# Local attention on Trainium2: query and value blocks laid out anew, two norms behind the evacuations, the last division in another bank

## The chip, the cores and the metric

The kernel runs on one core of a Trainium2 chip (trn2). The metric is the device time of one execution in microseconds, the median of several runs. Engine names are those of the profile: PE (TensorE, matrix multiply), PEld (its weight loads), DVE (VectorE), ACT (ScalarE), POOL (GpSimd), SP (the engine that issues most DMAs).

## The reference

Four layers are applied, one after the other, to an input `x` of shape (4, 56, 56, 128), each as `x = x + layer(group_norm(x))`. Layer 0 holds everything that the change touches: a local attention over windows of 7 x 7 pixels, then an attention over the whole image, then a two-layer perceptron. Shortened:

```python
# layer 0, on the group-normed x
xs = roll(x, (-3, -3))                       # shifted windows
wins = window_partition(xs)                  # (4*64, 49, 128)
x = roll(window_reverse(mha(wins)), (3, 3))  # local attention: 4 heads of 32
xf = x.reshape(4, 56*56, 128)
xf = xf + mha(layernorm(xf))                 # attention over the image
h = gelu(layernorm(xf) @ w1 + b1)
xf = xf + (h @ w2 + b2)
# mha: q, k, v = x@wq+bq, x@wk+bk, x@wv+bv per head;
#      softmax(q k^T / sqrt(32)) v, then @ wo + bo
```

Layer 1 is an edge network with 56 nodes in each row, layer 2 a spectral (Fourier) attention over all images with its own convolutions, layer 3 a convolution along one axis with sums along the other. All data are float32.

## The kernel before, in words

The program takes the four images one after the other through layers 0 and 1: `fast_layer` for layer 0, then `edge_layer`. While image b is in its local attention, steps of layer 2's norms for image b - 1 are strewn in between (not in image 0). After image 3, layers 2 and 3 are done for all images together.

Channels lie on the 128 partitions and the 3136 pixels of an image on the free axis, in the order of the windows: 64 windows of 49 pixels (`WIN`). The local attention, `fast_windows`, works in eight groups `g` of eight windows (`N` = 392 columns). One group passes through these stages:

- `norm`: the group-normed input of the group, `w_xg`. ACT makes it for groups 0 and 1 (L368), DVE for the others (L193, through `apply_norm`).
- `project`: TensorE multiplies `w_xg` with the query, key and value weights into three PSUM banks (L375, L376, L380; the value product separately for the four pairs of windows and the two windows, "parities", of a pair). Then the banks are emptied: queries head by head into `w_qd`, DVE for heads 0 and 2 (L225) and ACT for heads 1 and 3 (L223), keys by ACT into `w_kT` (L383), values by DVE for parity 0 (L232) and by ACT for parity 1 (L230) into `w_vd`.
- `score`: one matmul for each window multiplies its keys with the queries of all four heads (L394). `w_qd` is zero outside each head's 32 partitions, so that the four heads come apart. An exponential on ACT follows (L397), into `w_pT`.
- `value`: matmuls with `w_vd` (L409) give the weighted values, and in a 33rd column, which holds ones, the sum for the division (L412, L413).
- `turn`, `output`, `central`, `variance`: transposition, output weights, and the centring and squares of the next layer norm.

Three sets of the buffers `w_xg`, `w_kT`, `w_qd`, `w_vd`, `w_pT` rotate. They are cleared once an image by POOL, set by set: the tail of `w_xg` (L339), `w_qd` (L340), the tails of `w_kT` and `w_pT` (L341, L342), `w_vd` (L343) and the column of ones in `w_vd` (L345); the ones of a set come after the L340 of the next set.

PE, ACT and DVE follow the order in which the Python code issues their instructions, so the loop of `fast_windows` is the schedule. POOL's order is left to the framework. In turn n of the loop, the stages run for groups n + 2, n, n - 1 and so on: the norm of a group stands ahead of the projection of the group before the last, on DVE's queue too.

At the end of the eight groups come the layer norm's root and reciprocal (`root`, `invert`), the division `divide` (a matmul that spreads the inverse, L460, and a multiply on DVE, L461) and `attended`, which makes queries, keys (L468, L469) and values (L477, L479) of the attention over the image. Here `bank()` gives PSUM banks from two tags in turn, `w_mm` (three banks) and `w_late` (tag "acc", two banks), steered by the count `turns`. What is left of `divide` and `attended` runs inside the next stage, whose eight PSUM banks are one tile `f_pm`; its first scores go to banks 0 to 3 (L827), followed by exponentials (L830).

Of the kernel before, what the change touches and what calls it, by code (L numbers as in the profile page):

```python
# [12 lines left out]
F32 = mybir.dt.float32  # L13
# [6 lines left out]
P = 128  # L20
# [5 lines left out]
WIN = 49  # L26
# [6 lines left out]
def bc(ap, axis, n):  # L33

    ap = ap.unsqueeze(axis)
    shape = list(ap.shape)
    shape[axis] = n
    return ap.to_broadcast(shape)
# [181 lines left out]
def evac(k, i, out, ps, bias):  # L220

    if i % 2:
        k.nc.scalar.activation(out, ps, AF.Identity, bias=bias)  # L223
    else:
        k.nc.vector.tensor_scalar_add(out, ps, bias)  # L225


def copy(k, i, out, ps):
    if i % 2:
        k.nc.scalar.copy(out, ps)  # L230
    else:
        k.nc.vector.tensor_copy(out, ps)  # L232
# [74 lines left out]
def fast_windows(k, w, xw, xf, mr, shift, beside, Q, K, V, h1, inverse):  # L307
# [9 lines left out]
    nc, tc = k.nc, k.tc  # L317
    scale = 1.0 / math.sqrt(32.0)
    heads = [slice(32 * h, 32 * h + 32) for h in range(4)]
    halves = [slice(0, 64), slice(64, P)]  # L320
    N = 8 * WIN
# [4 lines left out]
    with ExitStack() as es:  # L326
        big = es.enter_context(tc.tile_pool(name="w_big", bufs=1))
# [5 lines left out]
        for i in range(BUFS):  # L333
            xg = big.tile([P, N + 16], F32, name="w_xg%d" % i)
            kT = big.tile([P, N + 16], F32, name="w_kT%d" % i)
            qd = big.tile([P, 8, 4, WIN], F32, name="w_qd%d" % i)
            vd = big.tile([P, 4, 4, 2, 33], F32, name="w_vd%d" % i)
            pT = big.tile([P, 16 * WIN + 16], F32, name="w_pT%d" % i)
            nc.gpsimd.memset(xg[:, N:], 0.0)  # L339
            nc.gpsimd.memset(qd, 0.0)  # L340
            nc.gpsimd.memset(kT[:, N:], 0.0)  # L341
            nc.gpsimd.memset(pT[:, 16 * WIN:], 1.0)  # L342
            nc.gpsimd.memset(vd, 0.0)  # L343
            for par in range(2):
                nc.gpsimd.memset(vd[halves[par], :, :, par, 32], 1.0)  # L345
            fixed.append((xg, kT, qd, vd, pT))
        outs, columns, squares, roots, chunk = {}, {}, {}, {}, 0
        eps = big.tile([P, 1], F32, name="w_eps")
# [2 lines left out]
        turns = 0  # L351

        def bank():
            nonlocal turns
            if source:
                return source[0]()
            turns += late
            if turns % 2:
                return psum.tile([P, 512], F32, tag="acc", name="w_late")
            return psum.tile([P, 512], F32, tag="mm", name="w_mm", bufs=3)  # L360
# [11 lines left out]
        def project(g):  # L372
            xg, kT, qd, vd, pT = fixed[g % BUFS]
            pq, pk, pv = bank(), bank(), bank()
            nc.tensor.matmul(pq[:, :N], w.wq, xg[:, :N], start=True, stop=True)  # L375
            nc.tensor.matmul(pk[:, :N], w.wk, xg[:, :N], start=True, stop=True)  # L376
            for i in range(4):
                for par in range(2):
                    t = (2 * i + par) * WIN
                    nc.tensor.matmul(pv[halves[par], i * P:(i + 1) * P], xg[:, t:t + 64], w.wv, start=True, stop=True)  # L380
            for h in range(4):
                evac(k, h, qd[heads[h], :, h, :], pq[heads[h], :N].rearrange("p (w t) -> p w t", t=WIN), w.bq[heads[h]])
            nc.scalar.activation(kT[:, :N], pk[:, :N], AF.Identity, bias=w.bk)  # L383
            for par in range(2):
                copy(k, par, vd[halves[par], :, :, par, 0:32],
                     pv[halves[par]].rearrange("p (a h d) -> p a h d", a=4, h=4))

        def score(g):
            xg, kT, qd, vd, pT = fixed[g % BUFS]
            ss = psum.tile([P, 2, 512], F32, tag="ss", name="w_ss", bufs=1)  # L390
            for i in range(4):
                for par in range(2):
                    v = 2 * i + par
                    nc.tensor.matmul(ss[halves[par], i // 2, i % 2 * 4 * WIN:(i % 2 + 1) * 4 * WIN],  # L394
                                     kT[:, v * WIN:v * WIN + 64], qd[:, v].rearrange("p h t -> p (h t)"),
                                     start=True, stop=True)
            nc.scalar.activation(pT[:, :16 * WIN].rearrange("p (a n) -> p a n", a=2), ss[:, :, :8 * WIN], AF.Exp,  # L397
                                 scale=scale, bias=k.wkeys)

        def value(g):  # L400
            xg, kT, qd, vd, pT = fixed[g % BUFS]
            o = wk.tile([P, 2, 2, 4, 32], F32, name="w_o", bufs=3)
            for a in range(2):
                po = psum.tile([P, 4, 2, 33], F32, tag="acc", name="w_po")
                for h in range(4):
                    for pp in range(2):
                        i = 2 * a + pp
                        c = (4 * i + h) * WIN
                        nc.tensor.matmul(po[halves[pp], h].rearrange("p b d -> p (b d)"), pT[:, c:c + 64],  # L409
                                         vd[:, i, h].rearrange("p b d -> p (b d)"), start=True, stop=True)  # L410
                rec = wk.tile([P, 4, 2], F32, name="w_rec")
                nc.vector.reciprocal(rec, po[:, :, :, 32])  # L412
                nc.vector.tensor_mul(o[:, a].rearrange("p b h d -> p h b d"), po[:, :, :, 0:32], bc(rec, 3, 32))  # L413
            outs[g] = o
# [33 lines left out]
        def root(i):  # L448
            nc.scalar.activation(inverse[:, i, :], roots[i][:, :N], AF.Sqrt, scale=1024.0, bias=eps)
            step(True)  # L450

        def invert(i):
            nc.vector.reciprocal(inverse[:, i, :], inverse[:, i, :])
# [31 lines left out]
        def step(root):  # L485
            nonlocal root_next
            if begun and (root or not root_next):
                root_next = next(steps, None) == "root"

        def run(*stages):  # L490
            for stage, g in stages:
                if 0 <= g < NG:
                    stage(g)
                    step(False)
# [4 lines left out]
        begun = False  # L499
        for n in range(NG + 1):  # L500
            begun = n > 1
            run((norm, n + 2), (project, n), (score, n - 1), (value, n - 2), (turn, n - 3), (output, n - 4),
                (central, n - 5), (variance, n - 6))
        variance(3)
        root(0)
        run((value, 7), (turn, 6), (output, 5), (central, 4))
        late = True
        run((turn, 7))
# [4 lines left out]
            pass  # L513
        root(1)
        nc.scalar.activation(eps, k.eps, AF.Exp)
        run((attended, 1), (divide, 2))
        invert(1)
        for _ in steps:
# [105 lines left out]
def fast_layer(k, w, xw, xf, x1, st, beside, mr, shift):  # L624
# [9 lines left out]
    with ExitStack() as es:  # L634
# [4 lines left out]
        oT = big.tile([P, TOK], F32, name="f_oT")  # L639
        inverse = big.tile([P, 2, 8 * WIN], F32, name="f_inverse")  # L640
        use = fast_windows(k, w, xw, xf, mr, shift, beside, qT, kT, va, oT, inverse)

        ring = es.enter_context(tc.tile_pool(name="f_ring", bufs=1)).tile([P, RING, NB], F32, name="f_ring")
# [2409 lines left out]
```

## Time and profile before

| what | value |
|---|---|
| time, median of 3 runs | 3447.18 us (3444.64 to 3448.79) |
| the profiled execution: time, span | 3464.64 us, 3462.8 us |
| mean granted TensorE clock | 0.991 |
| PE busy | 96% |
| DVE, ACT, POOL busy | 77%, 62%, 37% |
| local attention of images 0, 1, 2, 3 starts at (first L368) | 46.83, 676.60, 1310.80, 1946.98 us |
| first L830 after it | 118.22, 752.40, 1388.39, 2023.26 us |

The profile is of one execution, which the profiler makes slightly longer than the median. A row of the timeline has the start in us from the span's start, the duration, engine, line, operation, the program's tile names (output, then inputs), the shapes and the number of instructions merged into the row; in brackets stands how long the engine had been idle and what ended that. A float32 matmul appears as two records. PE's busy time counts pipelined matmuls whose ends are modelled, so that 96% does not mean that it runs at its peak.

### The profile page before, as it was taken

To read this page: it belongs to the slowest core of one execution; us is meant where nothing else is said; L and a number is where in the kernel's file an instruction comes from. 1 tells how busy PE (TensorE), PEld (TensorE's weight loads), DVE (VectorE), ACT (ScalarE), POOL (GpSimd) and SP (SyncE) were. 2 spreads that over 40 slices of the span, in tenths; PEclk is the share of its full clock that TensorE was granted. 3 is DMA by queue.
4 is the path that set the end of the run, shared out by engine and by line. 5 is a ranking of instruction groups with operands and counts; after the bars stand their busy time and mean duration, and the time that the engine had idled before them with its cause. 6 is when DMAs were issued, how large, how long until landed. Compare 5 with 4: busy or idle time off the path is not lost. (4 is left out here: it accounts for less than half of the span.)

```text
span 3462.8 us, 64536 instructions
## 1 busy us (share of the span) xinstructions
PE 3337.5 (96%) x27834; PEld 1441.2 (42%) x27834; DVE 2659.6 (77%) x2552; ACT 2134.9 (62%) x2257; POOL 1284.9 (37%) x795
## 2 busy tenths in 40 slices
PE   7999999999999999999999999999999999999998
PEld 4433333353333435333343443333337443346664
DVE  6588867868888696788859858887785878886756
ACT  4688876668888575788857568887654012215432
POOL 1000017700000490000019400001785978875766
PEclk9999999999999999999999999999999999999989
DMA  2243420024434000444310034342113057742201
GB/s 106 46 94 86 97 54 19 20 58 87 97 86 86 19 1 20 110 99 94 89 41 1 20 82 93 89 97 54 38 36 85 1 124 182 182 110 80 61 10 56
DMA packets 97868, 243.42 MB, mean 70 GB/s; under 512 B 64440, under 2 KB 69816, under 8 KB 92440
## 3 DMA queue, kind: packets, MB, share of 16 engines
q0 software_dynamic: 16128, 102.77, 14.8%
q1 hardware_dynamic: 74728, 123.61, 12.2%
q10 hardware_dynamic: 6720, 12.85, 1.3%
q8 instruction: 220, 3.60, 0.4%
q14 instruction: 72, 0.59, 0.1%
HBM read 79.43 MB, written 31.33 MB: 32 GB/s over the span
## 5 line engine op out<-in xcount | busy, mean ns | idle before, releaser
L830 ACT ACTIVATE f_ring<-f_pm 128x1792 f32<-128x1792 f32 (+1 forms) x764 | 1093.8, 1482 | 226.7 <-PE f_pm L827 179.2
L682 DVE TENSOR_TENSOR f_acc<-f_acc,f_ring 128x1792 f32<-128x1792 f32 x468 | 947.5, 2025 | 190.8 <-ACT f_ring L830 160.0
L827 PE MATMUL f_pm<-f_qT,f_kT 32*128 32x448 f32 x5376 | 722.8, 571 | 9.9 <-ACT f_p L716 4.1
L693 PE MATMUL f_pm<-f_ring,f_va 128*32 128x448 f32 (+1 forms) x6304 | 589.4, 490 | 0.0
L672 POOL DMA_DIRECT2D f_far<-f_ring x112 | 96.5, 862 | 1328.2 <-ACT f_ring L830 1027.0
L1275 POOL TENSOR_TENSOR e_tp<-e_a,e_c 128x1792 f32<-128x1792 f32 (+2 forms) x172 | 480.4, 2839 | 33.5 <-issue 33.4
L1273 DVE TENSOR_TENSOR e_td<-e_a,e_pc 128x1792 f32<-128x1792 f32 (+2 forms) x292 | 478.3, 1704 | 8.8 <-ACT e_c L1261 8.8
L827 PEld LDWEIGHTS f_pm<-f_qT,f_kT 32*128 32x128 f32 x5376 | 260.1, 183 | 411.8 <-ACT f_ring L830 301.1
L693 PEld LDWEIGHTS f_pm<-f_ring,f_va 128*32 128x32 f32 x6304 | 163.8, 109 | 410.1 <-issue 397.8
L1277 ACT ACTIVATE e_tp<-e_tp 128x1792 f32<-128x1792 f32 (+2 forms) x172 | 253.3, 1495 | 98.0 <-POOL e_tp L1275 98.0
L2040 DVE TENSOR_TENSOR u_ud<-u_px,u_d 112x1792 f32<-112x1792 f32 x144 | 263.4, 1863 | 39.9 <-PE u_po L2045 35.6
L2042 POOL TENSOR_TENSOR u_up<-xh,u_d 112x1792 f32<-112x1792 f32 (+1 forms) x72 | 240.9, 3374 | 56.0 <-PE u_po L2045 42.8
L1344 PE MATMUL e_acc<-e_td,t_edge 128*32 128x448 f32 x1952 | 231.6, 542 | 6.6 <-DVE e_td L1273 6.4
L2045 PE MATMUL u_po<-u_ud,AT 112*64 112x448 f32 x1056 | 212.4, 541 | 0.5 <-DVE u_ud L2040 0.5
L1344 PE MATMUL e_acc<-e_tp,t_edge 128*32 128x448 f32 x1184 | 148.0, 543 | 23.7 <-ACT e_tp L1277 23.6
L2045 PEld LDWEIGHTS u_po<-u_ud,AT 112*64 112x64 f32 x1056 | 74.0, 137 | 126.5 <-issue 112.3
L1344 PEld LDWEIGHTS e_acc<-e_td,t_edge 128*32 128x32 f32 x1952 | 61.8, 110 | 142.4 <-issue 94.2
L737 DVE RECIPROCAL f_den<-f_den 128x448 f32<-128x448 f32 x28 | 82.6, 2951 | 44.9 <-ACT f_den L734 44.9
L1874 POOL TENSOR_TENSOR q_u<-iS,q_g 128x1792 f32<-128x1792 f32 x32 | 104.3, 3287 | 12.2 <-PE q_acc L1889 12.2
L813 POOL TENSOR_TENSOR x<-xf,xw 128x343 f32<-128x343 f32 x28 | 25.5, 909 | 221.5 <-DVE xf L802 221.5
L2145 ACT COPY x_ev<-x_po 56x896 f32<-56x896 f32 x32 | 28.8, 900 | 126.7 <-DMA x_xs<-xat 57.8
L1889 PE MATMUL q_acc<-q_u,S 64*64 64x448 f32 x1024 | 101.2, 539 | 2.1 <-DVE y L1908 1.1
(538 smaller groups left out, 4622.3 us busy)
## 6 DMA issues: line engine op xcount, KB each, us to landing
f_far<-f_ring POOLq DMA_DIRECT2D x112, 896.0 KB, 6.4
u_d<-dd SPq DMA_DIRECT2D x46, 784.0 KB
f_far<-f_ring SPq DMA_DIRECT2D x28, 896.0 KB
xw<-in_x SPq DMA_DIRECT2D x4, 1568.0 KB
x2d<-x SPq DMA_DIRECT2D x4, 1568.0 KB
xat<-x SPq DMA_DIRECT2D x4, 1568.0 KB
x_xs<-xat ACTq DMA_DIRECT2D x32, 196.0 KB
xm<-x_ev ACTq DMA_DIRECT2D x64, 98.0 KB
```

Source lines behind the costliest of these rows:

```text
L682: nc.vector.tensor_add(e.acc, e.acc, slots(j, c))
L693: nc.tensor.matmul(e.po[heads[h], part], va[o, c, heads[h]], p, start=(c == 0), stop=(c == 23 and part.stop == NB))
L827: nc.tensor.matmul(ss[:, i, :NB], kT[heads[h], c * P:(c + 1) * P], qT[heads[h], blk(j)], start=True, stop=True)
L830: nc.scalar.activation(ring[:, slot:slot + m, :], ss[:, :m, :NB], AF.Exp, scale=scale)
L1273: nc.vector.tensor_tensor(t, am, cm, ALU.max)
L1275: nc.gpsimd.tensor_sub(t, am, cm)
L1277: nc.scalar.activation(tf, tf, AF.Relu)
L1344: nc.tensor.matmul(acc[quarters[r0 + r], :NB], w.S[:, 0, :], t[:, r].rearrange("p l n -> p (l n)"), start=(g == 0), stop=(g == len(turns) ...
L1874: nc.gpsimd.tensor_mul(u, bc(st.iS[:, bp, c, :HH], 1, HEADS), bc(g[:, n, c, :], 2, HH))
L2040: nc.vector.tensor_mul(u, bc(px[:, :, :NB], 2, m), dm)
L2042: nc.gpsimd.tensor_mul(u, bc(x, 2, m), dm)
L2045: nc.tensor.matmul(po[64 * b2:64 * b2 + 64, :NB], st.AT[:, 8 * i + h0 + q, 2 * bp + b2, :], u[:, b2, q, :], start=(left == 16), stop=(left ...
```

## The change

Four things are changed, all in `fast_windows`.

- `w_qd` has its heads outermost, (4 heads, 8 windows, 49) instead of (8, 4, 49). A head's evacuation then writes one unbroken run of 392 columns, and a window's score matmul reads four runs of 49.
- `w_vd` has its parities outermost, (2, 4, 4, 33) instead of (4, 4, 2, 33). The value matmul reads two runs of 33 instead of one of 66.
- In turns 0 and 1 of the loop, `project(n)` comes ahead of `norm(n + 2)`. On DVE, the norms of groups 2 and 3 then stand behind the evacuations of groups 0 and 1.
- `turns` is raised by one after `root(1)`, so that in `attended(1)` and `divide(2)` the tags `w_mm` and `w_late` change places. The last division's bank is then `w_late`'s bank 6 instead of `w_mm`'s bank 1.

No instruction is added or dropped.

```diff
-            qd = big.tile([P, 8, 4, WIN], F32, name="w_qd%d" % i)
-            vd = big.tile([P, 4, 4, 2, 33], F32, name="w_vd%d" % i)
+            qd = big.tile([P, 4, 8, WIN], F32, name="w_qd%d" % i)
+            vd = big.tile([P, 2, 4, 4, 33], F32, name="w_vd%d" % i)
...
-                nc.gpsimd.memset(vd[halves[par], :, :, par, 32], 1.0)
+                nc.gpsimd.memset(vd[halves[par], par, :, :, 32], 1.0)
...
-                evac(k, h, qd[heads[h], :, h, :], pq[heads[h], :N].rearrange("p (w t) -> p w t", t=WIN), w.bq[heads[h]])
+                evac(k, h, qd[heads[h], h], pq[heads[h], :N].rearrange("p (w t) -> p w t", t=WIN), w.bq[heads[h]])
             nc.scalar.activation(kT[:, :N], pk[:, :N], AF.Identity, bias=w.bk)
             for par in range(2):
-                copy(k, par, vd[halves[par], :, :, par, 0:32],
+                copy(k, par, vd[halves[par], par, :, :, 0:32],
                      pv[halves[par]].rearrange("p (a h d) -> p a h d", a=4, h=4))
...
-                    nc.tensor.matmul(ss[halves[par], i // 2, i % 2 * 4 * WIN:(i % 2 + 1) * 4 * WIN],
-                                     kT[:, v * WIN:v * WIN + 64], qd[:, v].rearrange("p h t -> p (h t)"),
+                    nc.tensor.matmul(ss[halves[par], i // 2, i % 2 * 4 * WIN:(i % 2 + 1) * 4 * WIN].rearrange("p (h t) -> p h t", h=4),
+                                     kT[:, v * WIN:v * WIN + 64], qd[:, :, v, :],
                                      start=True, stop=True)
...
-                        nc.tensor.matmul(po[halves[pp], h].rearrange("p b d -> p (b d)"), pT[:, c:c + 64],
-                                         vd[:, i, h].rearrange("p b d -> p (b d)"), start=True, stop=True)
+                        nc.tensor.matmul(po[halves[pp], h], pT[:, c:c + 64], vd[:, :, i, h, :], start=True, stop=True)
...
-            run((norm, n + 2), (project, n), (score, n - 1), (value, n - 2), (turn, n - 3), (output, n - 4),
+            run(*((norm, n + 2), (project, n))[::-1 if n < 2 else 1], (score, n - 1), (value, n - 2), (turn, n - 3), (output, n - 4),
                 (central, n - 5), (variance, n - 6))
...
         root(1)
         nc.scalar.activation(eps, k.eps, AF.Exp)
+        turns += 1
         run((attended, 1), (divide, 2))
```

## The prediction

> **What bounds the kernel now.** I read the page first, then the timeline around the first microseconds of each image's window stage, engine by engine, then the waits of that stretch, then the granted clock in short windows. The page says that TensorE is busy all the time:
>
> ```profile
> span 3462.8 us, 64536 instructions
> ...
> PE 3337.5 (96%) x27834; PEld 1441.2 (42%) x27834; DVE 2659.6 (77%) x2552; ACT 2134.9 (62%) x2257; POOL 1284.9 (37%) x795
> ```
>
> That share is an average. The change lies in the window stage alone, which runs four times for about 72 us, so what counts is which wait ends last there. Image 1, DVE's timeline (start, duration, engine, line, operation; in brackets the idle time before and its releaser):
>
> ```profile
> 677.20 3.61 DVE L193 TENSOR_SCALAR w_xg<-xw,mr 128x392 f32<-128x392 f32 x1
> 680.73 0.60 DVE L225 TENSOR_SCALAR w_qd<-w_mm,t_first 32x392 f32<-32x392 f32 x1
> 681.98 0.62 DVE L225 TENSOR_SCALAR w_qd<-w_mm,t_first 32x392 f32<-32x392 f32 x1 [0.65 <-ACT w_qd L223]
> 682.64 0.68 DVE L232 COPY w_vd<-w_mm 64x512 f32<-64x512 f32 x1
> 683.35 0.51 DVE L193 TENSOR_SCALAR w_xg<-xw,mr 128x392 f32<-128x392 f32 x1
> 684.32 0.61 DVE L225 TENSOR_SCALAR w_qd<-w_mm,t_first 32x392 f32<-32x392 f32 x1 [0.46 <-PE w_mm L375]
> ```
>
> Norm 2 (first line) takes 3.61 us where the same instruction takes 0.47 later, and the first evacuation of group 0 stands behind it. Its data were there at 678.86, when the first projection ended (L375 from 677.96, 0.90 us). POOL's timeline shows what held the norm:
>
> ```profile
> 676.72 1.41 POOL L340 MEMSET w_qd<- 128x1568 f32 x1
> ...
> 679.13 1.41 POOL L340 MEMSET w_qd<- 128x1568 f32 x1
> 680.47 0.40 POOL L345 MEMSET w_vd<- 64x16 f32 x2
> ...
> 681.99 1.41 POOL L340 MEMSET w_qd<- 128x1568 f32 x1
> 683.34 0.30 POOL L345 MEMSET w_vd<- 64x16 f32 x2
> ```
>
> Memsets follow each other without a gap; only ahead of L345 does POOL pause, and there, at 680.5, the norm gets through. The evacuations, which read PSUM, run at 0.60 to 0.62 us beside memsets. TensorE then stands still until the fourth head has been evacuated:
>
> ```profile
> 683.28 0.93 PE L375 MATMUL w_mm<-w_xg,t_first 128*128 128x392 f32 x2 [2.74 <-ACT w_qd L223]
> ```
>
> In image 2 the same hole is followed by a half clock for 6.8 us; in image 3 for 3.4 us, in images 0 and 1 not at all. Each row is a stretch with the busy time of PE, PEld, DVE, ACT and POOL; the granted clock is the third figure from the right:
>
> ```profile
> 1319.00:1320.00 1.00, 1.00 (x3) 0.28 (x1) 0.61 (x1) 0.09 (x1) 0.29 (x4) 0.50 0.00 0
> 1956.00:1957.00 1.00, 1.00 (x14) 1.00 (x12) 0.58 (x1) 0.39 (x1) 0.00 (x0) 0.50 0.00 0
> ```
>
> Does a delay there reach the end? The first exponential (L397) starts 12.77, 14.33 and 12.98 us after the first norm of images 1, 2 and 3, and the first score exponential of the next stage (L830) 75.80, 77.59 and 76.28 after it: the delay is kept and grows slightly. From that L830 to the next image's first norm it is 558.38, 558.40 and 558.59 us. So the path is rigid, and a microsecond at the front is one at the end.
>
> [...]
>
> **The change part by part.**
>
> *Norms.* One DVE instruction each is moved for n = 0 and 1, in four images; no DMA and no other queue is moved. Image 1, from the first norm at 676.60 as zero. h0 to h3 are the four head evacuations, DVE and ACT in turn. The projection ends at 2.26, and h0 starts 0.11 later, as it does at other groups: 2.37 instead of 4.13. The distances of the trace (0.64, 0.61, 0.66) put h3 at 4.28 and the value copy of DVE at 4.28 to 4.96; only then comes norm 2, in the midst of the next run of memsets. It gets in at the next pause, ahead of the second L345; without norm 2 in the first pause POOL gets there about 0.1 earlier (image 0 needs 2.82 from pause to pause, image 1 2.93): 6.69, and the norm ends 0.24 later, as the earlier ones did. Then h0 of group 1 starts at 6.85, instead of 7.72: **0.87 us gained**, not the whole 1.76, since the norm now blocks group 1 instead of group 0. On ACT, h3, the key evacuation, the copy (0.6 each) and the table load (1.28) follow, and the first exponential starts at 11.89 instead of 12.77: 0.88. What is late next is that norm. Norms 3 and 4 then stand one behind the other ahead of h0 of group 2: 0.48 more, hidden by the exponential and h1 behind it (1.4 us of slack); without that cover 0.48 an image. Three images: 2.64.
>
> Image 0 gains little: there norm 2 got in at once (ended at 48.56; the projection ended at 48.52), and it was norm 3 that sat from 51.27 to 53.90 behind memsets. Norm 2 takes its place. POOL, no longer held up by it (L341 took 0.21 and L343 0.16 longer there than in image 1), is up to 0.37 earlier: I take 0.2.
>
> *Clock.* The hole of 2.74 us becomes 1.0 (L380 of group 0 ends at 3.93, L375 of group 1 starts h3 plus 0.64 = 4.92), as image 0 has it (1.0 and 1.24), and image 0 shows no dip. The dips cost 77.59 − 75.80 = 1.79 and 76.28 − 75.80 = 0.48: 2.3 us gained. Ends: 0, if they come all the same, and 5.4, if an execution without the profiler has all three.
>
> *Layouts.* Evacuations write the same elements: 0.620 us into separated runs for w_qd, 0.624 for the unbroken xf of line L225 on more partitions. ACT likewise, 0.585 and 0.593. Value copies keep 16 runs of 32. The score matmul now reads four runs of 49 columns, the value matmul two of 33. Two rows of the last stage read broken runs: 392 columns in 7 runs 487 ns (L2309), 448 in 14 runs 536 ns (L2345); unbroken ones are 492 (L375) and 541 (L2045). I take nothing; bounds below.
>
> *Banks.* Before, the first scores stand 0.75 us behind the division's multiply:
>
> ```profile
> 117.00 1.03 PE L827 MATMUL f_pm<-f_qT,f_kT 32*128 32x448 f32 x8 [0.75 <-DVE f_oT L461]
> ```
>
> The division moves to bank 6, outside banks 0 to 3 of these scores. But the new score tile spans all eight banks, and in the built program its first matmul waits for the same count of DVE, the multiply, as before. The other waits move among steps that are over 1 us old. So nothing; if the wait did go, 0.7 an image.
>
> Sum for the profiled execution: 2.64 + 0.2 + 2.3 = 5.1 off a span of 3462.8 (own time 3464.64, 17.5 above the median of 3447.18). For the median I carry the same 5: 3442.2. A measurement of this kernel tells about 0.2%, or 6.9 us, from no change: the bounds are 3440.3 and 3454.1.
>
> **The rivals.**
> - *Earlier hand-over:* [...] Then h0 of group 1 starts at 5.93, 0.9 more in three images: 3439.5. Against it: four of five blocked norms sat until the pause.
> - *The scores leave the division:* 4 x 0.7 more, 3439.4. Speaks against it: the wait count.
> - *The layouts undo the alternation of DVE and ACT:* ACT waits 57.6 us in total for DVE's evacuations; half of it on the path would give 3413. Against it: both still read one bank, and each still waits for the other's count.
> - *Slower: broken runs cost TensorE.* Place: L394 and L409, where group follows group and TensorE has no gap (16.00 of 16.00 us at 70.80 to 86.80). A group has 8 serial score streams with 3 breaks and 16 value streams with 1: 40, or 1280 in all. At 10 ns a break that is 12.8 us, less 4.9: 3455. From 4 ns it eats the gain, from 9 it is slower by over 0.2%. The two rows above speak against it.
> - *Nothing or little comes of it:* norm 2 sits until the last memset (h0 of group 1 1.0 later in images 1 to 3, 1.7 in image 0, less the clock's 2.3: 3449.5), or the dips fall elsewhere: 3447.
>
> **How the numbers follow.** Main case 0.50, of which 0.15 below 3440.3 (more dips without the profiler than with it); earlier hand-over 0.16; freed scores 0.10; alternation undone 0.04; broken runs 0.10; little or nothing 0.10. Faster by over 0.2%: 0.15 + 0.16 + 0.10 + 0.04 = 0.45; slower 0.10; within 0.45. The main case alone spans 3439 to 3445; with the first two rivals and the last one the range is 3436.5 to 3448, which leaves out the alternation, the broken runs and tails.
>
> **What would show it.** After the change, L225 of group 0 starts some 2.4 us after the first L368 in images 1 to 3, an L193 of 1.5 to 2 us stands ahead of group 1, L375 of group 1 shows an idle time of about 1 us, the first L397 starts near 11.9, no half clock follows, L394 and L409 keep 329 and 222 ns, L827 keeps its 0.75. The prediction is wrong if the second L193 lasts beyond 3 us, if L394 grows, or if the 558.4 us from L830 to the next image change.

## The result, and the profile after

| | before | after |
|---|---|---|
| median of 20 runs each | 3449.93 us (3444.32 to 3464.32) | 3443.12 us (3440.56 to 3447.76) |
| ratio after / before | | 0.9978, 95% interval 0.9970 to 0.9986 |
| span of the profiled execution | 3462.8 us | 3441.5 us |
| mean granted clock of it | 0.991 | 0.997 |

The changed kernel is faster by 0.22% by this ratio; the two medians lie 6.8 us, or 0.20%, apart. The two profiled spans differ by 21.3 us, and most of that is not the change. The two rows below, of the windows of before and then of after, show a stretch of the last stage, far behind the edited code. The columns are stretch, length, busy time of PE, PEld, DVE, ACT and POOL, granted clock, share of the DMA engines and GB/s:

```profile
3300.00:3320.00 20.00, 18.53 (x93) 13.60 (x92) 10.75 (x31) 8.26 (x13) 7.99 (x6) 0.58 0.00 1
```

```profile
3300.00:3320.00 20.00, 19.45 (x166) 15.32 (x166) 14.35 (x31) 11.37 (x13) 12.75 (x10) 1.00 0.01 1
```

The profiled execution of before happened to run there at about half the clock (0.58, and 0.56 in the next 20 us). From the first L2292 to the last instruction it took 349.9 us against 334.8 after: 15.1 of the 21.3. The first L2292 itself starts 6.2 us earlier (3106.7 against 3112.9). So 6.2 is what the change and its surroundings account for in this pair. It also corrects a sentence of mine above: nothing here shows that the profiler makes an execution longer (after's took 3443.31, its median is 3443.12). Before's, at 3464.64, was one with a long dip, a stretch at half the clock, and two others of the 20 runs of before took as long (3464.26 and 3464.32).

DVE's timeline of after, image 1, where the first L368 starts at 675.99:

```profile
678.36 0.61 DVE L225 TENSOR_SCALAR w_qd<-w_mm,t_first 32x392 f32<-32x392 f32 x1 [1.68 <-PE w_mm L375]
679.62 0.62 DVE L225 TENSOR_SCALAR w_qd<-w_mm,t_first 32x392 f32<-32x392 f32 x1 [0.65 <-ACT w_qd L223]
680.27 0.68 DVE L232 COPY w_vd<-w_mm 64x512 f32<-64x512 f32 x1
680.99 1.91 DVE L193 TENSOR_SCALAR w_xg<-xw,mr 128x392 f32<-128x392 f32 x1
682.82 0.60 DVE L225 TENSOR_SCALAR w_qd<-w_mm,t_first 32x392 f32<-32x392 f32 x1
```

The evacuation no longer stands behind a norm: it waits for the projection (1.68 us, released by L375) and starts 2.37 after the first L368. Norm 2 now comes fourth and lasts 1.91 us. POOL's timeline shows beside which memsets it got in:

```profile
681.27 1.41 POOL L340 MEMSET w_qd<- 128x1568 f32 x1
682.62 0.51 POOL L345 MEMSET w_vd<- 64x16 f32 x2
```

It is again at L345, as in the kernel before, one set later: the norm ends 0.22 us behind the end of the L340 (682.90 against 682.68), and the pair of L345 takes 0.51 us, where an undisturbed one takes 0.29 or 0.30. In the kernel before it ended 0.27 behind the L340 (680.81 against 680.54), beside a pair of 0.40. The pause ahead of L345 that the prediction speaks of is not in the rows of either kernel: L345 starts 0.06 or 0.07 us before the L340 ahead of it ends. PE's timeline has the hole behind the evacuations of group 0, and the windows of the two places where the clock had dipped (images 2 and 3) follow it:

```profile
680.91 0.93 PE L375 MATMUL w_mm<-w_xg,t_first 128*128 128x392 f32 x2 [0.98 <-ACT w_qd L223]
```

```profile
1316.00:1326.00 10.00, 8.65 (x104) 5.93 (x102) 6.84 (x22) 7.76 (x11) 1.65 (x8) 1.00 0.01 2
1948.00:1960.00 12.00, 10.65 (x120) 7.28 (x120) 8.84 (x25) 8.40 (x13) 3.03 (x9) 1.00 0.01 1
```

0.98 us idle instead of 2.74, and a full clock at both places. The milestones, in us after the first L368 of each image, read from ACT's timeline:

| | image 0 | image 1 | image 2 | image 3 |
|---|---|---|---|---|
| first L397, before | 12.02 | 12.77 | 14.33 | 12.98 |
| first L397, after | 11.85 | 11.85 | 11.85 | 11.84 |
| first L830, before | 71.39 | 75.80 | 77.59 | 76.28 |
| first L830, after | 71.17 | 74.85 | 74.85 | 74.86 |
| gain at L830 | 0.22 | 0.95 | 2.74 | 1.42 |

The sum is 5.33. The stage of image 0 also starts 0.41 earlier, ahead of all edits. Of the rest of the 6.2 us, 0.1 lies in the three stretches from an L830 to the next image's first L368, and 0.4 between the last L830 and the first L2292, behind all edits; what shortened those I do not know.

### The profile page after: what moved, and what is told of

Its sections match the earlier page's. It is cut to its first block, busy times and chain, and to the rows that moved or that the text cites. A ratio compares the mean times of both kernels' runs of the same rounds, so it can differ in the third digit from the quotient of the medians.

```text
span 3441.5 us, 64526 instructions
## 1 busy us (share of the span) xinstructions
PE 3317.2 (96%) x27834; PEld 1425.6 (41%) x27834; DVE 2651.4 (77%) x2552; ACT 2134.0 (62%) x2257; POOL 1284.9 (37%) x795
## 5 line engine op out<-in xcount | busy, mean ns | idle before, releaser
L830 ACT ACTIVATE f_ring<-f_pm 128x1792 f32<-128x1792 f32 (+1 forms) x764 | 1093.8, 1482 | 226.6 <-PE f_pm L827 179.1
L827 PE MATMUL f_pm<-f_qT,f_kT 32*128 32x448 f32 x5376 | 722.8, 571 | 9.9 <-ACT f_p L716 4.1
L827 PEld LDWEIGHTS f_pm<-f_qT,f_kT 32*128 32x128 f32 x5376 | 260.1, 183 | 411.8 <-ACT f_ring L830 301.1
```

The lines of the kernel that those rows point to most:

```text
L827: nc.tensor.matmul(ss[:, i, :NB], kT[heads[h], c * P:(c + 1) * P], qT[heads[h], blk(j)], start=True, stop=True)
L830: nc.scalar.activation(ring[:, slot:slot + m, :], ss[:, :m, :NB], AF.Exp, scale=scale)
```

## The experiments

Each is an edit of the kernel before, unless it says otherwise. "At clock 0.997" means the median of those runs alone whose mean granted clock was 0.997; in the runs of before and of the change one thousandth of mean clock goes with 2 to 3 us on average (in the last group 3450.51 at 0.995 and 3444.36 at 0.998 before, 3449.09 and 3441.24 after), so this takes most of the clock's chance out of a comparison. The clock is recorded to a thousandth, so a difference of 1 or 2 us can remain. Three groups of runs, each on one chip, had the kernel before beside them: e1 to e4 (before 3450.74), e5 to e8 (3446.36), e9 to e11 (3449.15).

### e1: the order of the norms alone

```diff
-            run((norm, n + 2), (project, n), (score, n - 1), ...
+            run(*((norm, n + 2), (project, n))[::-1 if n < 2 else 1], (score, n - 1), ...
```

> Only the order of norm and projection in turns 0 and 1 is changed; blocks and banks are those of before. If the whole gain comes from the norms (my theory), the first exponential (L397) starts 11.85 us after the first L368 in images 1 to 3, as with the full change, no half clock follows, and the time is 6 to 8 us below before (ratio 0.9978, as the full change). If the layouts or the banks bring a share, the ratio stays above 0.9985.

Measured: 3445.81 us, ratio 0.9988 (0.9978 to 0.9997). The first L397 comes at 11.87 to 11.89 in all four images and the first L830 at 71.25, 74.91, 74.92 and 74.93, within 0.1 us of the changed kernel. DVE's timeline of image 1 is the changed kernel's, down to the norm:

```profile
681.16 1.91 DVE L193 TENSOR_SCALAR w_xg<-xw,mr 128x392 f32<-128x392 f32 x1
```

So in the traces this one line carries the gain; the other three edits are left 0.06 to 0.08 us an image. The times are less clear: 4.9 us between the medians instead of the 6 to 8 expected, and a ratio above the 0.9985 that was to speak for a share of the layouts or banks. But the interval reaches down to the change's 0.9978, and at clock 0.997 this run is 4.5 us below before (3442.72 of 4 runs against 3447.22 of 5), no less than the change is (3.5, in the last group).

### e2: the two layouts alone

```diff
-            qd = big.tile([P, 8, 4, WIN], F32, ...)
-            vd = big.tile([P, 4, 4, 2, 33], F32, ...)
+            qd = big.tile([P, 4, 8, WIN], F32, ...)
+            vd = big.tile([P, 2, 4, 4, 33], F32, ...)
```

with the evacuations and matmuls that go with them, as in the change.

> Only the two block layouts are changed; order and banks are those of before. My theory: nothing, within 1.5 us of before; L225 of w_qd keeps 620 ns, L394 329 ns, L409 222 ns, and ACT still waits about 57 us in total for DVE's head evacuations. Rival (broken runs cost TensorE): L394 or L409 longer, time above before by more than 3 us. Rival (the layouts let DVE and ACT evacuate side by side): that wait falls below 20 us and the time falls by 5 us or more.

Measured: 3450.21 us, ratio 0.9994 (0.9984 to 1.0005), no difference. The groups of instructions of e2, which have the total busy time and mean ns behind the bar:

```profile
L394 PE MATMUL w_ss<-w_qd,w_kT 128*64 128x196 f32 x512 | 48.3, 329 | 1.4 <-ACT w_pT L397 1.4
...
L223 ACT ACTIVATE w_qd<-w_mm,t_first 32x392 f32<-32x392 f32 x64 | 37.1, 579 | 58.1 <-DVE w_qd L225 58.0
L409 PE MATMUL w_po<-w_vd,w_pT 128*64 128x66 f32 x1024 | 35.6, 221 | 0.0
```

and the same groups of before:

```profile
L394 PE MATMUL w_ss<-w_qd,w_kT 128*64 128x196 f32 x512 | 49.7, 337 | 1.4 <-ACT w_pT L397 1.4
...
L223 ACT ACTIVATE w_qd<-w_mm,t_first 32x392 f32<-32x392 f32 x64 | 37.4, 584 | 57.7 <-DVE w_qd L225 57.6
L409 PE MATMUL w_po<-w_vd,w_pT 128*64 128x66 f32 x1024 | 35.8, 222 | 0.0
```

The 337 contains matmuls at half clock (so does the 329 here, fewer); the median of an L394 is 329 ns before and 328 here. Reading four runs of 49 costs TensorE nothing here (328 ns), writing one run instead of eight saves ACT 5 ns of 584, and ACT waits for DVE as long as ever (58.0 against 57.6 us): the alternation is not undone by the layout. In image 1, which has a full clock in both, L830 comes at 75.74 against 75.80.

### e3: the banks alone

```diff
         nc.scalar.activation(eps, k.eps, AF.Exp)
+        turns += 1
         run((attended, 1), (divide, 2))
```

> Only the exchange of the last banks; order and layouts are those of before. My theory: nothing, within 1.5 us of before, and the first scores (L827) of each image still stand 0.75 us behind the division's multiply. Rival (the scores no longer wait for the division): that idle time goes and the time falls by about 2.8 us.

Measured: 3448.77 us, ratio 0.9995 (0.9987 to 1.0003), no difference. What L827 (here L828) waits for, us and times:

```profile
  DVE f_oT L461: 3.0, 4
```

Still the division's multiply, 3.0 us over the four images, as in the changed kernel and in before. The bank of the division is not what the scores wait for.

### e4: the hole filled, the delay left in

In images 1 to 3 three matmuls of ones, whose product is never read, follow the first value projection:

```diff
+            if g == 0 and relieved:
+                fill = psum.tile([P, 512], F32, tag="acc", name="w_fill")
+                for _ in range(3):
+                    nc.tensor.matmul(fill[:, :3 * P], k.ones, bc(k.ones, 1, 3), start=True, stop=True)
```

> Order, layouts and banks of before; after the value product of group 0 in images 1 to 3, three matmuls of ones (384 columns each) into a bank that is free then fill the hole of 2.74 us; their product is never read. If the half clock follows from the hole, no stretch of half clock is left in the first 20 us of images 1 to 3, the first L397 starts at 12.77 us in all three, as in the undisturbed image 1 of before, and the time falls by what the dips cost on average, about 2.3 us (ratio near 0.9993). Rival (the clock falls for another reason): dips of 3 to 7 us are still there and L397 scatters from 12.8 to 14.3.

Measured: 3449.80 us, ratio 1.0002 (0.9991 to 1.0012). PE's timeline, image 1:

```profile
679.06 2.20 PE L384 MATMUL w_fill<-c_ones 128*128 128x384 f32 x6
681.87 0.93 PE L375 MATMUL w_mm<-w_xg,t_first 128*128 128x392 f32 x2 [0.61 <-ACT w_qd L223]
```

No half clock follows in any image: L830 comes at 75.79, 75.79 and 75.82, where before had 75.80, 77.59 and 76.28. One trace alone could be luck, but the other kept traces say the same. The hole of 2.73 to 2.75 us stands in images 1 to 3 of before, e2, e3 and e7. In nine of these twelve images a half clock begins within it or up to 1.4 us behind it. The windows of e2, images 2 and 3, have a clock of 0.50:

```profile
1317.20:1320.20 3.00, 2.78 (x4) 1.17 (x4) 1.38 (x3) 1.68 (x4) 1.93 (x9) 0.50 0.00 0
1952.20:1955.20 3.00, 2.67 (x4) 1.17 (x4) 1.49 (x3) 1.68 (x4) 2.03 (x9) 0.50 0.00 0
```

No half clock stands there in the 36 images whose longest hole in the first 12 us is about 1.3 us or less (1.32 in image 0 of before and of the change; they are all of the change, e1, e4, e5, e6, e9, e10 and e11, and image 0 of before, e2, e3 and e7). The dips cost 2.3 us in the trace of before, 1.6 in e2, 2.2 in e3 and, at the first L397, 2.8 in e7. So in these traces the dips come with the hole: in nine of twelve images with it, in none of 36 without. In e4's own times the 2.3 us do not show: its ratio is 1.0002, though the interval still holds the 0.9993 expected. At clock 0.997 it is level with before (3447.01 of 6 runs against 3447.22 of 5), as a comparison at equal clock has to be; 6 of its 14 runs reach that clock against 6 of 43 of before, and two took 3464 us or more at 0.992. Where the clock of those other runs fell, no trace shows. That the dips come with the hole is shown; how, and what they are worth in the median, is not.

### e5 and e6: norms that do not wait for POOL

e5 is before, e6 is the changed kernel, both with norms 2 and 3 made by an instruction that reads two tensors from SBUF; `mr` and `shift` are what ACT's norm uses already.

```diff
+            elif g < 4:
+                nc.vector.scalar_tensor_tensor(out, x, mr[:, 1:2], shift.to_broadcast([P, N]), ALU.mult, ALU.add)
```

> Order, layouts and banks of before; the norms of groups 2 and 3 (DVE) are written as x times scale plus a broadcast shift, an operation with two inputs in SBUF, instead of tensor_scalar. [...] norm 2 and norm 3 take about 0.56 us each in all images, the first evacuation of group 0 starts 2.4 us after the first L368 in images 1 to 3 and that of group 1 at about 5.96 instead of 7.72 (before) and 6.83 (the change), the first exponential at about 11.0 (image 0: 10.4). Time 8 to 10 us below before, ratio 0.9973. Rival (the norms wait for something else, such as the load of the image or a clearing of their buffer): they still take 2 to 3.6 us and the time is that of before.

> The full change, with the norms of groups 2 and 3 written as in e5. [...] the wait of group 1 goes: first evacuation of group 1 at about 5.96, first exponential at about 11.0, 0.85 us less in each of images 1 to 3 and 1.5 in image 0 than the change: about 4 us below the change, ratio to before 0.9967. If order no longer counts [...], e5 and e6 agree within 1.5 us.

Measured: e5 3438.49 us, ratio 0.9977 (0.9969 to 0.9985); e6 3440.50 us, ratio 0.9988 (0.9979 to 0.9997). DVE's timeline of e5, image 1, with the order of before:

```profile
674.64 0.62 DVE L370 SCALAR_TENSOR_TENSOR w_xg<-xw,mr,shift 128x392 f32<-128x392 f32 x1
676.40 0.61 DVE L225 TENSOR_SCALAR w_qd<-w_mm,t_first 32x392 f32<-32x392 f32 x1 [1.14 <-PE w_mm L377]
...
679.04 0.63 DVE L370 SCALAR_TENSOR_TENSOR w_xg<-xw,mr,shift 128x392 f32<-128x392 f32 x1
680.00 0.61 DVE L225 TENSOR_SCALAR w_qd<-w_mm,t_first 32x392 f32<-32x392 f32 x1 [0.33 <-PE w_mm L377]
```

and POOL's, beside it:

```profile
674.16 1.41 POOL L340 MEMSET w_qd<- 128x1568 f32 x1
...
675.60 0.99 POOL L343 MEMSET w_vd<- 128x1056 f32 x1
```

The same norm of the same data, at the same place and beside the same memsets, takes 0.62 us instead of 3.61. So it was not DVE's place in the queue alone that cost time but the instruction with which the norm is made: the tensor_scalar sat beside POOL's memsets, the scalar_tensor_tensor did not. That it would not was my assumption ahead of the run; why the one waits and the other does not, no run shows. Group 1 is evacuated 5.96 us after the first L368 (7.72 before, 6.83 after the change), and the first exponential comes at 11.02.

e6's median lies 2.0 us above e5's, where level within 1.5 us was one expectation and 4 us below the change the other. Four of its 22 runs took over 3454 us at a clock of 0.993; at clock 0.997 the two are 0.9 apart (3439.44 of 10 runs, 3438.53 of 9). The traces have e6 0.08 to 0.09 us ahead at each first L830. So the order no longer counts, as e9 to e11 test once more.

### e7: the last division moved behind the first scores

```diff
-        run((attended, 1), (divide, 2))
+        run((attended, 1))
...
-    rest = [((attended, 2),), ((divide, 3),)] + ...
+    rest = [((divide, 2), (attended, 2)), ((divide, 3),)] + ...
```

> Order, layouts and banks of before; the division of group 2 (divide(2)) is issued after the first scores of the next stage instead of ahead of them. If the first scores (L827) wait for the last step that uses any bank of the old stage, they now wait for the value copy instead of the multiply and start 0.7 us earlier in every image: 2.8 us below before, ratio 0.9992, less what attended(2) loses by the later division. Rival (the wait is hidden anyway, since the first exponential waits for something else): the time does not change.

Measured: 3468.32 us, ratio 1.0065 (1.0047 to 1.0084), 22 us slower, where 2.8 us less had been expected. DVE's timeline behind the first scores, image 1:

```profile
750.78 2.59 DVE L453 RECIPROCAL f_inverse<-f_inverse 128x392 f32<-128x392 f32 x1
...
753.94 2.48 DVE L193 TENSOR_SCALAR x<-x,s_mr 128x784 f32<-128x784 f32 x4
756.33 0.56 DVE L461 TENSOR_TENSOR f_oT<-f_oT,f_pm 128x392 f32<-128x392 f32 x1
```

and PE's, waiting for that multiply:

```profile
756.94 1.68 PE L468 MATMUL f_pm<-f_oT,w_fq 128*128 128x392 f32 x2 [4.16 <-DVE f_oT L461]
```

The scores did leave the division: the first L830 comes 0.71 us earlier in image 0 (70.68), and 62.40 instead of 63.03 us after the first L397 in image 1. But the multiply now stands behind a reciprocal of 2.59 us and four steps of layer 2's norms (2.48 together) on DVE. TensorE idles 4.16 us and then runs at half clock (0.50 in the window from 756 to 761; 1.68 us for a pair that takes 0.93). From the first L830 to the next image's first L368 image 1 takes 565.61 instead of 558.40 us.

### e8: single columns

```diff
-            qd = big.tile([P, 8, 4, WIN], F32, ...)
+            qd = big.tile([P, 4, WIN, 8], F32, ...)
...
-                ... qd[:, v].rearrange("p h t -> p (h t)"),
+                ... qd[:, :, :, v],
```

Each window's columns then lie 8 elements apart, in the evacuations' writes and in the score matmul's reads.

> Order and banks of before, value block as before; the query block has the window innermost, so that a score matmul reads 196 columns that are 32 bytes apart, 195 breaks instead of 3 in the change. If a break costs TensorE time, L394 grows by over 1 ns a break (329 ns to 500 and more) and the time rises by 10 us or more; my theory: L394 keeps 327 to 330 ns and the time is that of before within 2 us, unless the evacuations, which now write single elements, become slower: L225 and L223 of w_qd stay at 620 and 585 ns if they do not.

Measured: 3493.58 us, ratio 1.0129 (1.0113 to 1.0146). The groups of e8:

```profile
L394 PE MATMUL w_ss<-w_qd,w_kT 128*64 128x196 f32 x512 | 96.2, 532 | 0.4 <-ACT w_pT L397 0.4
...
L223 ACT ACTIVATE w_qd<-w_mm,t_first 32x392 f32<-32x392 f32 x64 | 61.3, 958 | 70.6 <-DVE w_qd L225 70.5
L225 DVE TENSOR_SCALAR w_qd<-w_mm,t_first 32x392 f32<-32x392 f32 x64 | 58.4, 912 | 47.9 <-ACT w_qd L223 34.3 <-PE w_mm L375 13.3 <-POOL w_vd L345 0.2
```

A pattern can cost, against my expectation: L394 grows from 329 to 532 ns, an evacuation by half or more (from 584 to 958 ns on ACT, from 612 to 912 on DVE). L394's busy time rises by 46.5 us (96.2 − 49.7), and the kernel by 47.2. That the two are so close is chance, for more than one thing differs. The evacuations grew too, and norm 2 took 1.14 us instead of 3.61, although order and memsets are those of before. DVE's and POOL's timelines of e8, image 1:

```profile
687.81 1.14 DVE L193 TENSOR_SCALAR w_xg<-xw,mr 128x392 f32<-128x392 f32 x1
689.57 0.92 DVE L225 TENSOR_SCALAR w_qd<-w_mm,t_first 32x392 f32<-32x392 f32 x1 [0.62 <-PE w_mm L375]
```

```profile
687.32 1.41 POOL L340 MEMSET w_qd<- 128x1568 f32 x1
688.67 0.33 POOL L341 MEMSET w_kT<- 128x16 f32 x1
688.72 0.30 POOL L342 MEMSET w_pT<- 128x16 f32 x1
688.76 1.15 POOL L343 MEMSET w_vd<- 128x1056 f32 x1
```

The norm starts 0.49 us behind the first L340, as in before (0.48), but gets in behind that memset and not at an L345: it ends 0.22 us behind it (688.95 against 688.73), with L341 next on POOL, and so in images 2 and 3. The first evacuation comes 2.36 us after the first L368, not 4.13. Which of the two places a norm gets in at is therefore not settled by the order of the instructions; what settles it, no run shows. At the four first L830 e8 is 42.9 us behind before, dips included. How much of that is the score matmuls and how much the evacuations was not separated. The dear case is an element at a time (532 ns); runs of 49, as in the change, cost nothing (328 ns, e2).

### e9, e10, e11: the change, the other norms, and both, on one chip

e9 is the changed kernel, e10 is e5 and e11 is e6 again.

> The changed kernel itself, beside the next two on one chip, so that they can be set against each other. Predicted from its first runs: ratio 0.998 to the kernel before, and a first exponential 11.85 us behind the first L368 in images 1 to 3.

> Kernel before with norms 2 and 3 as scalar_tensor_tensor (two tensors from SBUF, the second one the shift's column spread over the row), once more on the chip of the changed kernel. Theory (the norm's wait behind POOL's memsets is the whole front cost, and the order of the norms is one of two ways round it): the first exponential comes at 11.02, so this is faster than the changed kernel by 0.8 us an image, 2.5 to 3 in all, a ratio of 0.9991 to it (0.997 to the kernel before). Rival (its lead in the run before was chance of the clock): level with the changed kernel.

> Changed kernel with norms 2 and 3 as scalar_tensor_tensor. Theory: with the wait gone the order of the norms is worth only what the layouts give, 0.04 to 0.09 us an image, so this is level with the kernel before carrying the same norms (within 0.5 us at equal clock). Rival (the change brings something of its own beside the norms): faster than that one by 2 us or more.

| | median | ratio to before | at clock 0.997 | first L397, image 1 |
|---|---|---|---|---|
| before | 3449.15 | | 3446.21 (5 runs) | 12.77 (profile of before) |
| e9, the change | 3442.66 | 0.9982 (0.9976 to 0.9989) | 3442.68 (8) | 11.85 |
| e10, other norms | 3437.82 | 0.9973 (0.9963 to 0.9983) | 3437.82 (5) | 11.02 |
| e11, both | 3437.96 | 0.9971 (0.9961 to 0.9982) | 3438.87 (3) | 10.98 |

With norms that need not wait, the old order beats the change by 4.8 us in the median, and adding the change to it brings nothing that these runs can tell: two ways round one wait, which don't add up. The first L830 says the same: 74.83 in image 1 for the change, 74.06 for e10, 73.97 for e11. e10 and e11 are the fastest kernels here. The traces explain 3.7 us of their lead over the change (1.34 in image 0, and 0.77 to 0.79 in each of the others). At clock 0.998 e10 leads by 3.6 us (3437.66 of 2 runs against 3441.24 of 7); the 1.1 us beyond that in the medians is no more than a clock given to a thousandth leaves open.

## Why the prediction was right

*Where the delay was, and what held it.* Right. The step from "3.61 us where 0.47 would do" to a norm shut out by memsets was an inference from two timelines; e5 bears it out by changing the norm's instruction and nothing else (0.62 us beside the same memsets). Too strong was the sentence that the norm gets through only ahead of L345, where POOL pauses. In image 0 of before norm 2 got in behind the first L340 (the norm ended at 48.56, the memset at 48.34), and in images 1 to 3 of e8 it did so too.

*0.87 us an image, not 1.76.* Right, and it was the finer half of the argument: the norm was moved, not freed, and blocks group 1 in place of group 0. Predicted: evacuation of group 0 at 2.37, of group 1 at 6.85, first exponential at 11.89. Measured: 2.37, 6.83, 11.85. The undisturbed image 1 gained 0.92 at its first L397 (0.88 predicted) and 0.95 at its first L830. Part of this is luck: that norm 2 would sit until the second L345, and not get in between two memsets as in e8, was the likelier case by count (four of five) and had no further reason. The rival "Earlier hand-over", in which norm 2 gets in between two memsets as in image 0, for 0.9 us more in three images, was closer than it looked. The predicted cover for norms 3 and 4 held: they stand together at 685.44 and the exponential was not late.

*Image 0, 0.2.* Measured 0.17 at L397, 0.22 at L830.

*Clock, 2.3.* Right for the profiled pair: image 2 gained 1.79 and image 3 0.47 more than image 1. The four traces with the hole lost 1.6 to 2.8 us to these dips, 2.2 in the mean, those without it nothing. How a hole of 2.73 to 2.75 us (2.3 in e8) brings a dip, and why not in every image, no run shows. For the median, which I let carry the same 2.3, the runs show less exactly. At clock 0.997 the change is worth 3.5 us (3446.21 to 3442.68 in the last group); norms in three images and image 0 were put at 2.84, and the traces give 3.07 at L830 without the dips (at clock 0.998 the times give 3.1). The other 3.0 of the 6.5 us between the medians go with a clock that is a thousandth higher after the change (0.997 against 0.996). That is near the size predicted, and e4 shows where it can come from, but e4 did not reproduce the gain in its own median. So the clock's share of the median fits, and is not shown.

*Layouts, 0.* Right within 0.06 us an image. The rival of broken runs is refuted by e2 (328 ns for an L394, against 329); e8 shows the price it imagined, in a pattern that the change doesn't have.

*Banks, 0.* Right by the waits of e3 and of the changed kernel. The rival's size, 0.7 us if the scores came off the division, was right as well (e7: 0.63 and 0.71). But e7 frees the scores by issuing the division later, which the rival did not mean, and the division is then late for its next reader, at a cost ten times as large.

*The path is rigid.* Right: 558.40, 558.36 and 558.53 us from L830 to the next first L368 after the change.

*The sum.* 5.1 predicted, 5.33 at the four L830, 6.2 up to the last stage, 6.8 and 6.5 in the medians. The predicted time of 3442.2 lies 0.9 below the measured median, but it was counted from the median of three runs, 3447.18; the median of before over 20 runs is 3449.93. Counted from that, the sum is 1.7 us short, and the closeness of 0.9 is luck: a start that was 2.8 us too low made up for it. Wrong too, without weight in the sum, was the remark that an execution under the profiler is slower.

## What to carry to other kernels

When an instruction takes many times its usual duration, ask what other engine was running, and look for the place at which it got in; then ask what it will hold up at its new place before you book the whole delay as gain. Moving it behind urgent work got half of the delay back here (group 1 at 6.83 instead of 7.72); another instruction for the same norm, which took 0.62 us beside the same memsets, got all of it (group 1 at 5.96), for 0.15 us more busy time. And before a step is moved off the path, read what stands ahead of it in the new queue, and who waits for it there.

## What the runs showed of the hardware that I had not expected

- The quicker instruction is the dearer one here: the tensor_scalar takes 0.47 us in groups 4 to 7 (median in e5) and, for norm 2 beside POOL's memsets, 3.61 (before) or 1.14 (e8, at the same place), the scalar_tensor_tensor 0.62 beside them (e5).
- Idle stretches of TensorE of 2.3 to 2.75 us in this stage came with a half clock in 12 of 16 images (before, e2, e3, e7, e8), as one of 4.16 us did in e7; where the longest was about 1.3 us or less, none was seen in 36 images.
- The cost of a broken pattern is not counted in breaks: four runs of 49 columns read at the speed of one run of 196 (328 against 329 ns), while single columns 32 bytes apart take 532 ns.
